# Flamingo block with gated cross attention and hyper-connections: the high part of normalized x made by ScalarE from x itself, and five finished weight and value tiles as row tiles of the tail

## The chip, the cores and the metric

The kernel runs on one core of a Trainium2 chip. The metric is the device time of one execution in microseconds (us). The engines are PE (TensorE; its weight loads are PEld), DVE (VectorE), ACT (ScalarE), POOL (GpSimd) and SP (SyncE, which issues nearly all transfers). L275 means line 275 of the kernel.

## What is computed

The reference takes x of 8 batches, 512 rows d and 2048 columns s, and a context of the same shape. Two gated steps follow each other:

```python
x = x + tanh(g_xattn) * xattn(layernorm(x), ctx, mask, ...)
x = x + tanh(g_ffn)   * ffn(layernorm(x), ...)
```

- xattn: in patches of 128 columns, q and k come from the normalized x by 256x512 weights, the values from the context; 8 heads of 32 attend within a patch; gelu, an output projection and the mask follow.
- ffn: each row of 2048 is four streams of 512. From the normalized row come 16 + 4 + 4 logits. The 16 become a 4x4 mixing matrix by 50 Sinkhorn iterations (temperature 0.1), blended with the identity; the others are softmaxed to weights `H_pre` and `H_post`. The output is the mixed streams plus `H_post` times a 512x512 branch of the `H_pre` sum.

Everything is float32. The layer norm runs along s, so its mean and scale belong to a row d, which is a partition of a tile.

## The kernel before

The main loop walks over 32 blocks of 512 columns (4 per batch), each in four steps t of one patch; a string of letters (`ORDER`) fixes which pieces are emitted in each step. These pieces are prepared up to three blocks ahead. The order on each engine's queue is not the program's: the launch code builds with a scheduler that simulates a timeline (`schedule_with_timeline_sim=True`, L1210) and takes the pieces by priority, mostly that of program order, as their inputs and buffers come free. Tiles of one tag share as many buffers as `bufs` says, and a new tile of that tag waits until the oldest is free.

What the change and the steps of the prediction touch:

- `proj(n)` (L260): q and k of block n. Each product is made of float16 parts: normalized x is split into a high part xh and a low part xl = xn - xh, and PE adds three products per chunk of 128 rows (L288 to L290). For each of the 4 chunks c, POOL makes xn = x * rstd + nb in float32 (L270; ACT does so for two chunks of the first block, L268), ACT casts xn to float16 (L275), and POOL subtracts (L277; DVE for the two). xn has `BUF_XNP` = 2 buffers, xh and xl have `BUF_XHP` = 4 each. ACT and DVE then take the result from PSUM as two halves (L292, L293).
- `vproj` (L322) makes the values of two patches with the weights `Wv` into `VF[0]` or `VF[1]`; `attv` (L626) reads them. `smax`, `expo` (L333, L614) make the scores, `mh` (L350) carries the row maximum back to the stacked q.
- `outp` (L648): gelu on ACT, o times the mask on POOL (L658), transposes (L667), the output projection and x1 = x + its result, stored to memory.
- `ffn` (L741): the Sinkhorn chain of a batch on DVE (sums and reciprocals) and POOL (products, L870 and L876; DVE for the last batch), with an exponential on ACT every ten sweeps. It ends in `Et` and, for TensorE's chunks, a copy through memory into `HR` (L911, L913).
- The mix of a batch: four chunks of 128 rows, each either on VectorE (`mixv`, L935) or on TensorE (`mixp`, L983). `PE_MIX` gives TensorE one chunk of batch 4, all of batches 5 and 6 and three of batch 7. These 12 chunks are emitted after the main loop, in the tail, with the rest of VectorE's chunks.
- In `mixp` a chunk is read again as 4 tiles xc of 128x512 (SP, L995), ACT adds the mean (L996), PE makes the weighted sum (L997), ACT copies it out (L1000), PE transposes it (L1004), `branch` splits it by ACT and DVE (L927, L928) and multiplies (L931 to L933), ACT copies it out (L1015). Then for each of 4 groups g PE adds two products in PSUM (L1030, L1031), ACT writes the row tile w with a bias (L1033), and SP stores it (L1034). The row tile takes turns: even g in the tag "e32" (2 buffers, which hold the exponentials in the main loop), odd g in the tag "eh" (1 buffer).

Of the kernel before, what the change touches and what calls it, by code (L numbers as in the profile page):

```python
# [9 lines left out]
F32 = mybir.dt.float32  # L10
# [3 lines left out]
AF = mybir.ActivationFunctionType  # L14
# [5 lines left out]
P = 128  # L20
# [19 lines left out]
BUF_GP = 1  # L40
BUF_OP = 1
BUF_XHP = 4
BUF_XNP = 2
BUF_XTP = 4
BUF_CTP = 2
BUF_QDP = 3
# [14 lines left out]
BUF_W = 2  # L61
# [3 lines left out]
BUF_EP = 2  # L65
BUF_XPRE = 1
PSTEPS = (0,1,1,2)
SP0 = 1
XH_POOL = lambda c: False
CAP = 1.0  # L70
NORM0 = True
D_MH = 0
# [26 lines left out]
def gated_xattn_mhc_kernel(  # L99
# [21 lines left out]
    V, A, G, T, SY = nc.vector, nc.scalar, nc.gpsimd, nc.tensor, nc.sync  # L121
# [6 lines left out]
    def ctile(shape, dt, name):  # L128
        return const.tile(shape, dt, tag=name, name=name)
# [16 lines left out]
    WqkH = ctile([P, 4, 512], F16, "WqkH")  # L146
    WqkL = ctile([P, 4, 512], F16, "WqkL")
    Wv = ctile([P, 4, DK], F32, "Wv")
# [35 lines left out]
    xsp = ctx.enter_context(tc.tile_pool(name="xsp", bufs=2))  # L184
    xnp = ctx.enter_context(tc.tile_pool(name="xnp", bufs=BUF_XNP))
    xhp = ctx.enter_context(tc.tile_pool(name="xhp", bufs=BUF_XHP))
# [3 lines left out]
    ep = ctx.enter_context(tc.tile_pool(name="ep", bufs=BUF_EP))  # L190
# [6 lines left out]
    VF = [ctile([P, 2, DK], F32, f"VF{i}") for i in range(NV)]  # L197
# [5 lines left out]
    def defer(k, tag, fn):  # L203
        if k == 0:
            fn()
        else:
            late.append([k, fn, tag])
# [13 lines left out]
    rstd1 = {}  # L221
    nb1 = {}
# [37 lines left out]
    def proj(n):  # L260

        b, k = divmod(n, NBLK)
        xt = xtile[n]
        hs, ls = [], []
        for c in range(4):
            xn = xnp.tile([P, BLK], F32, tag="xn", name="xn")
            if n == 0 and c > 1:
                A.activation(xn, xt[c], AF.Identity, scale=rstd1[b][:, c : c + 1], bias=nb1[b][:, c : c + 1])  # L268
            else:
                G.tensor_scalar(xn, xt[c], rstd1[b][:, c : c + 1], nb1[b][:, c : c + 1], ALU.mult, ALU.add)  # L270
            h = xhp.tile([P, BLK], F16, tag="xh", name="xh")
            if XH_POOL(c):
                G.tensor_copy(h, xn)
            else:
                A.copy(h, xn)  # L275
            l = xhp.tile([P, BLK], F16, tag="xl", name="xl")
            (V if n == 0 and c > 1 else G).tensor_tensor(l, xn, h, ALU.subtract)  # L277
            hs.append(h)
            ls.append(l)
        if NORM0:  # L280
            yield
        qd = qdp.tile([2, 4, 2, P, BLK], F16, tag="qd", name="qd")
        qds[n] = qd
        for m in range(4):
            ps = ps_p.tile([P, BLK], F32, tag="p", name="qk")
            ms = slice(m * P, (m + 1) * P)
            for c in range(4):
                T.matmul(ps, WqkH[:, c, ms], hs[c], start=(c == 0), stop=False)  # L288
                T.matmul(ps, WqkH[:, c, ms], ls[c], start=False, stop=False)  # L289
                mm = T.matmul(ps, WqkL[:, c, ms], hs[c], start=False, stop=(c == 3))  # L290
            ev = evp.tile([P, 2, BLK], F16, tag="ev", name="ev")
            ae = A.activation(ev[:, 0, :], ps, AF.Identity, bias=bqs[:, m : m + 1])  # L292
            ve = V.scalar_tensor_tensor(ev[:, 1, :], ps, bqs[:, m : m + 1], ev[:, 0, :], ALU.add, ALU.subtract)  # L293
            defer(D_QD, "qd", lambda m=m, ev=ev: SY.dma_start(qd[m // 2, 0:2, m % 2].rearrange("t p s -> p t s"), ev))
            if n == LASTN and m == LASTM:
                last.update(pe=mm, act=ae, dve=ve)
            yield
# [59 lines left out]
    with tc.tile_pool(name="set", bufs=1) as st:  # L357
# [99 lines left out]
        for _ in proj(0):  # L457
            pass
# [24 lines left out]
        with tc.issue_after(sd_[0].ins):  # L483
            load_x(NBLK)
        ctload(1)
        pj = proj(1)
        for _ in range(4 if NORM0 else 3):
            next(pj)
# [61 lines left out]
    fp = ctx.enter_context(tc.tile_pool(name="fp", bufs=2))  # L550
# [366 lines left out]
    def mix(b, maps):  # L917
        E, cst, pre, prc, post, rec, HR = maps
        for c in range(4):
            if c in PE_IN[b - B]:  # L920
                yield from mixp(b, c, maps, True)
            elif c not in PE_MIX[b - B]:
                yield from mixv(b, c, maps)

    def branch(pt, ph, pl, y):

        A.copy(ph, pt)  # L927
        V.tensor_tensor(pl, pt, ph, ALU.subtract)  # L928
        yield 1
        for e in range(4):  # L930
            T.matmul(y, ph[:, e, :], WbH[:, e, :], start=(e == 0), stop=False)  # L931
            T.matmul(y, ph[:, e, :], WbL[:, e, :], start=False, stop=False)
            T.matmul(y, pl[:, e, :], WbH[:, e, :], start=False, stop=(e == 3))  # L933

    def mixv(b, n, maps):  # L935
# [31 lines left out]
        for i in range(4):  # L967
# [12 lines left out]
            defer(D_OUT if live[0] else 0, "out", lambda i=i, w=w: SY.dma_start(out[b, n * P : (n + 1) * P, 512 * i : 512 * i + 512], w))  # L980
            yield 1

    def mixp(b, n, maps, inp=False):  # L983

        E, cst, pre, prc, post, rec, HR = maps
        rows = x1s[b].rearrange("d (j e) -> (d j) e", j=4)
        orow = out[b].rearrange("d (j e) -> (d j) e", j=4)
        PD = f1.tile([P, 4, 32], F32, tag="PD", name="PD", bufs=2)
        G.tensor_tensor(PD, blk.unsqueeze(1).broadcast_to([P, 4, 32]), rec[:, 4 * n : 4 * n + 4, 0:1].broadcast_to([P, 4, 32]), ALU.mult)
        xc = []  # L990
        xps = (ps_t if inp else ps_p).tile([P, 512], F32, tag="t" if inp else "p", name="xpp")
        for g in range(4):
            q = 4 * n + g
            t = fp.tile([P, 512], F32, tag="x1", name="xc", bufs=BUF_X1) if inp else xp_.tile([P, 512], F32, tag="xt", name="xc")
            SY.dma_start(t, rows[q * P : (q + 1) * P, :])  # L995
            A.activation(t, t, AF.Identity, bias=rec[:, q, 1:2])  # L996
            T.matmul(xps[32 * g : 32 * g + 32, :], PD[:, g, :], t, start=True, stop=True)  # L997
            xc.append(t)
        xs = fp.tile([P, 512], F32, tag="xpre", name="xps", bufs=BUF_XPRE) if inp else xp_.tile([P, 512], F32, tag="xt", name="xps")
        A.copy(xs, xps)  # L1000
        yield 1
        pt = (ps_t if inp else ps_p).tile([P, 4, P], F32, tag="t" if inp else "p", name="xpT")
        for e in range(4):
            T.transpose(pt[:, e, :], xs[:, e * P : (e + 1) * P], ident)  # L1004
        y = ps_t.tile([P, 512], F32, tag="t", name="yp")
        if inp:
            ph = fp.tile([P, 4, P], F16, tag="ph", name="ph", bufs=BUF_PH)
            pl = fp.tile([P, 4, P], F16, tag="pl", name="pl", bufs=BUF_PH)
        else:
            ph = xhp.tile([P, 4, P], F16, tag="xh", name="phb")  # L1010
            pl = xhp.tile([P, 4, P], F16, tag="xl", name="plb")
        for r in branch(pt, ph, pl, y):
            yield r
        ys = fp.tile([P, 512], F32, tag="pj", name="ys", bufs=BUF_PJ) if inp else xp_.tile([P, 512], F32, tag="xt", name="ys")
        A.copy(ys, y)  # L1015
        yield 1
        QD = xtp.tile([P, P, 4], F32, tag="xTt", name="QD")
        G.tensor_tensor(QD, ident.unsqueeze(2).broadcast_to([P, P, 4]), post[:, n, :].unsqueeze(1).broadcast_to([P, P, 4]), ALU.mult)
        HD = xtp.tile([P, 4, 32, 4], F32, tag="xTt", name="HD")
        G.tensor_tensor(  # L1020
            HD,
            blk.unsqueeze(1).unsqueeze(3).broadcast_to([P, 4, 32, 4]),
            HR[:, 4 * n : 4 * n + 4, :].unsqueeze(2).broadcast_to([P, 4, 32, 4]),
            ALU.mult,
        )
        pw = None if inp else [ps_s.tile([P, 2, 512], F32, tag="s", name="mx") for _ in range(2)]
        for g in range(4):
            q = 4 * n + g
            ps = ps_t.tile([P, 512], F32, tag="t", name="mx1") if inp else pw[g // 2][:, g % 2]
            T.matmul(ps, QD[:, 32 * g : 32 * g + 32].rearrange("p t i -> p (t i)"), ys, start=True, stop=False)  # L1030
            T.matmul(ps, HD[:, g].rearrange("p t i -> p (t i)"), xc[g], start=False, stop=True)  # L1031
            w = fp.tile([P, 512], F32, tag="w", name="w", bufs=BUF_W) if inp else ep.tile([P, 512], F32, tag="eh" if g % 2 else "e32", name="wp", bufs=1 if g % 2 else BUF_EP)
            A.activation(w, ps, AF.Identity, bias=rec[:, q, 2:3])  # L1033
            SY.dma_start(orow[q * P : (q + 1) * P, :], w)  # L1034
            yield 1
# [178 lines left out]
```

## Time and profile before

| what | us |
|---|---|
| median of 3 runs | 1701.85 |
| lowest and highest run | 1693.76, 1705.0 |
| the profiled execution, its own time | 1693.74 |
| span in its trace | 1692.0 |
| main loop's last values product (L642) | 1487.64 |
| first row tile of the tail (L1033) | 1516.05 |
| Sinkhorn of batch 6 ends (store of Et, L911) | 1590.97 |
| Sinkhorn of batch 7 ends (store of Et, L911) | 1645.06 |
| last store issued (L980) | 1689.05 |

The profile is of one execution; times inside it count from the start of its span. A line of the waits reads: engine and line that stood idle, what released it, us in total, times, the longest. A line of the timeline reads: start, duration, engine, line, operation, output and inputs, and in brackets the idle time before it and what ended that. A group of instructions gives count, busy time, mean duration in ns and the idle time ahead of it.

### The profile page before, as it was taken

What the parts mean: (1) busy time and instruction counts of PE and PEld (TensorE: products, weight loads), DVE (VectorE), ACT (ScalarE), POOL (GpSimd) and SP (SyncE); (2) the same over time, 40 slices, a digit from 0 to 9 for tenths busy, and PEclk for the clock granted to TensorE, in tenths of its full rate; (3) what the DMA queues carried; (4) which work ended last, traced back from release to release, by engine and by line L of the source; (5) the groups of instructions that cost most, each with busy time, mean ns of one, the idle gap of its engine ahead of it and who ended that gap; (6) DMA issues with size and microseconds to landing.
All of it is one profiled execution on the core that took longest, in us unless ns stands there. A gap on an engine that the chain in (4) does not pass through costs nothing.

```text
span 1692.0 us, 32528 instructions
## 1 busy us (share of the span) xinstructions
PE 1487.1 (88%) x10453; PEld 880.8 (52%) x10517; DVE 1201.6 (71%) x3552; ACT 1065.3 (63%) x2046; POOL 818.6 (48%) x1158
## 2 busy tenths in 40 slices
PE   4899989999997988988898988888798999778887
PEld 2555546556655655555555554545455556543233
DVE  7634334666776679868777777777788889878872
ACT  3356475667657666686568765686566667555454
POOL 1322233544454465656466654656557655643211
PEclk9899999999999999999999999999999999899999
DMA  6789897787588556876589664876556575334443
GB/s 202 206 234 276 252 257 182 199 242 219 158 240 232 168 173 196 258 228 204 151 237 281 204 176 137 260 230 179 172 164 203 179 206 148 96 107 143 135 157 125
DMA packets 317656, 330.61 MB, mean 195 GB/s; under 512 B 50535, under 2 KB 215719, under 8 KB 317486
## 3 DMA queue, kind: packets, MB, share of 16 engines
q1 hardware_dynamic: 316238, 328.20, 66.0%
q8 instruction: 83, 1.36, 0.4%
q14 instruction: 87, 0.71, 0.1%
q10 hardware_dynamic: 1248, 0.33, 0.1%
HBM read 226.71 MB, written 101.16 MB: 194 GB/s over the span
## 4 chain that ended last, share of the span: by engine, by line
PE 38%; DVE 20%; DMA 14%; ACT 10%; issue 9%; POOL 8%; SPq 1%; another core or an unknown queue 0%; POOLq 0%; ACTq 0%; DVEq 0%
PE vp L330 5%; DMA xs<-in_x_dram 4%; PE qk L288 3%; PE qk L290 3%; PE qk L289 3%; DVE w L976 3%; PE op L693 2%; DMA out_dram<-w 2%; PE lgx L564 2%; PE op L694 2%; PE op L695 2%; PE u L642 2%; PE u L638 2%; PE smax L340 2%; DMA xt<-in_x_dram 2%
## 5 line engine op out<-in xcount | busy, mean ns | idle before, releaser
L330 PE MATMUL vp<-Wv,ct 128*128 128x256 f32 x1024 | 253.0, 398 | 17.5 <-DMA ct<-in_cx_dram 8.7
L330 PEld LDWEIGHTS vp<-Wv,ct 128*128 128x128 f32 x1024 | 198.0, 199 | 54.4 <-DMA ct<-in_cx_dram 9.5
L876 POOL TENSOR_TENSOR W<-E,uv 128x64 f32<-128x64 f32 x343 | 115.6, 340 | 220.4 <-DVE uv L874 86.3
L976 DVE SCALAR_TENSOR_TENSOR w<-x,Et,w 128x512 f32<-128x512 f32 x180 | 182.8, 1017 | 34.0 <-POOL w L974 24.7
L288 PE MATMUL qk<-xh,WqkH 128*128 128x512 f16 x512 | 196.9, 386 | 11.2 <-DVE ev L293 8.6
L277 POOL TENSOR_TENSOR xl<-xn,xh 128x512 f16<-128x512 f32 x126 | 155.3, 1243 | 97.3 <-ACT xh L275 96.0
L289 PE MATMUL qk<-xl,WqkH 128*128 128x512 f16 x512 | 197.3, 386 | 2.9 <-POOL xl L277 2.9
L290 PE MATMUL qk<-xh,WqkL 128*128 128x512 f16 x512 | 197.3, 385 | 0.0
L870 POOL TENSOR_TENSOR W<-E,uv 128x64 f32<-128x64 f32 x308 | 105.3, 345 | 165.6 <-DVE uv L880 70.9
L343 DVE TENSOR_REDUCE smax<-smax 128x8 f32<-128x1024 f32 x128 | 156.2, 1221 | 39.4 <-PE smax L340 32.3
L623 ACT ACTIVATE e<-sT,ebi,esc 128x1024 f32<-128x1024 f32 x128 | 153.6, 1200 | 22.1 <-PE sT L621 21.9
L878 DVE TENSOR_REDUCE sm<-W 128x16 f32<-128x64 f32 x392 | 99.7, 257 | 84.9 <-POOL W L876 80.2
L293 DVE SCALAR_TENSOR_TENSOR ev<-qk,bqs,ev 128x512 f16<-128x512 f32 x128 | 94.3, 738 | 57.5 <-ACT ev L292 56.5
L693 PE MATMUL op<-gh,WoH 128*128 128x512 f32 x256 | 119.3, 468 | 17.5 <-DVE ev L293 9.5
L699 ACT ACTIVATE junk<-xt,nmean 128x512 bf16<-128x512 f32 x128 | 92.0, 719 | 66.9 <-DVE xt L697 30.4
L270 POOL TENSOR_SCALAR xn<-xt,ln_r,nb 128x512 f32<-128x512 f32 x126 | 115.5, 920 | 36.5 <-DVE nb L254 28.2
L292 ACT ACTIVATE ev<-qk,bqs 128x512 f16<-128x512 f32 x128 | 86.8, 679 | 66.8 <-PE qk L290 66.3
L658 POOL TENSOR_TENSOR o<-o,mb 128x1024 f32<-128x1024 f32 x32 | 76.0, 2375 | 100.0 <-ACT o L653 99.3
L872 DVE TENSOR_REDUCE sm<-W 128x16 f32<-128x64 f32 x352 | 74.4, 214 | 58.9 <-POOL W L870 55.4
L974 POOL TENSOR_TENSOR w<-w,pj 128x512 f32<-128x512 f32 x60 | 78.3, 1306 | 75.4 <-ACT w L969 42.9
L340 PE MATMUL smax<-KS,QS 97*128 97x128 f16 x1024 | 86.5, 226 | 31.4 <-ACT mh L350 14.2
L697 DVE TENSOR_TENSOR xt<-op,xt 128x512 f32<-128x512 f32 x128 | 86.9, 679 | 36.6 <-remote 22.6
(289 smaller groups left out, 3503.3 us busy)
## 6 DMA issues: line engine op xcount, KB each, us to landing
xt<-in_x_dram SPq DMA_DIRECT2D x128, 256.0 KB
ct<-in_cx_dram SPq DMA_DIRECT2D x64, 512.0 KB
qd<-ev SPq DMA_DIRECT2D x128, 256.0 KB
xTt<-in_xT_dram SPq DMA_DIRECT2D x128, 256.0 KB
x1s<-xt SPq DMA_DIRECT2D x128, 256.0 KB
xs<-in_x_dram SPq DMA_DIRECT2D x112, 256.0 KB
QS<-qd SPq DMA_DIRECT2D x192, 128.0 KB
KS<-qd SPq DMA_DIRECT2D x192, 128.0 KB
```

Of the source, the lines that this page charges most:

```text
L270: G.tensor_scalar(xn, xt[c], rstd1[b][:, c : c + 1], nb1[b][:, c : c + 1], ALU.mult, ALU.add)
L277: (V if n == 0 and c > 1 else G).tensor_tensor(l, xn, h, ALU.subtract)
L288: T.matmul(ps, WqkH[:, c, ms], hs[c], start=(c == 0), stop=False)
L289: T.matmul(ps, WqkH[:, c, ms], ls[c], start=False, stop=False)
L290: mm = T.matmul(ps, WqkL[:, c, ms], hs[c], start=False, stop=(c == 3))
L330: T.matmul(ps[:, h, :], ct[:, c, h * P : (h + 1) * P], Wv[:, c, :], start=(c == 0), stop=(c == 3))
L340: T.matmul(sc[:, h, :], q[0:97, h, sl], kk[0:97, h, sl], start=True, stop=True)
L343: V.tensor_reduce(mx, sc, AX.X, ALU.max)
L623: A.activation(e32, sc, AF.Exp, bias=ebi[:, t : t + 1], scale=esc[:, t : t + 1])
L693: T.matmul(ps, WoH[:, e, cs], gh[:, e], start=(e == 0), stop=False)
L876: (G if SK_POOL(b - B + 8) else V).tensor_tensor(W4[:, h], E4[:, h], ub[:, h], ALU.mult)
L976: V.scalar_tensor_tensor(w, x1[j], E[:, n, 4 * j + i : 4 * j + i + 1], w, ALU.mult, ALU.add)
```

## The change

There are two parts. In `proj` the high part xh is no longer a cast of xn: ACT computes x * rstd + nb from x and writes it as float16, so it does not depend on xn. POOL still makes xn and the difference. xn has one buffer instead of two; an unused switch goes.

In `mixp`, for chunks of the tail, the row tile w comes from a rota of eight instead of the two tags: half of `WqkH` and of `WqkL` seen as float32, half of `Wv`, `VF[0]`, `VF[1]`, then "eh" once and "e32" twice. The five tiles hold weights and values that the main loop reads and the tail does not.

```diff
-BUF_XNP = 2
+BUF_XNP = 1
...
-XH_POOL = lambda c: False
...
             h = xhp.tile([P, BLK], F16, tag="xh", name="xh")
-            if XH_POOL(c):
-                G.tensor_copy(h, xn)
-            else:
-                A.copy(h, xn)
+            A.activation(h, xt[c], AF.Identity, scale=rstd1[b][:, c : c + 1], bias=nb1[b][:, c : c + 1])
...
+    spare = [WqkH.bitcast(F32)[:, 0:2, :], WqkL.bitcast(F32)[:, 0:2, :], Wv[:, 0:2, :], VF[0], VF[1]]
+    turn = [0]
+
+    def tailw(g):
+        k = turn[0] % (len(spare) + 3)
+        turn[0] += 1
+        if k < len(spare):
+            return spare[k].rearrange("p c e -> p (c e)")
+        return ep.tile([P, 512], F32, tag="eh" if k == len(spare) else "e32", name="wp", bufs=1 if k == len(spare) else BUF_EP)
...
-            w = fp.tile([P, 512], F32, tag="w", name="w", bufs=BUF_W) if inp else ep.tile([P, 512], F32, tag="eh" if g % 2 else "e32", name="wp", bufs=1 if g % 2 else BUF_EP)
+            w = fp.tile([P, 512], F32, tag="w", name="w", bufs=BUF_W) if inp else tailw(g)
```

## The prediction

> **What bounds the kernel now.** I read the page's totals and slices first, then the chain that ended last, then the waits by engine for 300 to 1400 us, then the tail after the main loop.
>
> ```profile
> PE 1487.1 (88%) x10453; PEld 880.8 (52%) x10517; DVE 1201.6 (71%) x3552; ACT 1065.3 (63%) x2046; POOL 818.6 (48%) x1158
> PE   4899989999997988988898988888798999778887
> ACT  3356475667657666686568765686566667555454
> PE 38%; DVE 20%; DMA 14%; ACT 10%; issue 9%; POOL 8%; SPq 1%; another core or an unknown queue 0%; POOLq 0%; ACTq 0%; DVEq 0%
> ```
>
> PE is busy in eight or nine tenths of nearly every slice and carries the largest part of the chain; ACT is busy 63% and carries 10%, POOL 48% and 8%. No single engine is saturated: PE is held up by many short waits. So work that is moved between ACT and POOL is worth what PE waits for it, not what it lasts. These are the waits around the changed lines, over the whole span (us, times, longest):
>
> ```profile
> POOL xl L277 <- ACT xh L275: 96.0, 29, 17.0
> ACT xh L275 <- POOL xn L270: 19.9, 18, 2.5
> PE smax L340 <- ACT mh L350: 14.2, 9, 3.8
> PE vp L330 <- ACT VF L331: 6.1, 4, 2.6
> PE qk L289 <- POOL xl L277: 2.9, 4, 1.1
> PE qk L288 <- ACT xh L275: 1.2, 1, 1.2
> ```
>
> POOL stands 96.0 us at the subtraction for the high part, and ACT 19.9 us for the normalized row, but PE waits only 2.9 + 1.2 = 4.1 us for either part. The waits by window say that 77.1 of the 96.0 us fall before 300 us, where POOL has little else (57.98 us busy from 100 to 300 us); 19.0 us are left from 300 to 1400 us.
>
> In the tail TensorE's chunks go through PE, ACT and the store. Here is ACT, and then SP's queue, in one chunk:
>
> ```profile
> 1654.22 0.69 ACT L1033 ACTIVATE wp<-mx,rec 128x512 f32<-128x512 f32 x1 [0.17 <-PE mx L1031]
> 1656.38 0.69 ACT L1033 ACTIVATE wp<-mx,rec 128x512 f32<-128x512 f32 x1 [0.99 <-PE mx L1031]
> 1659.21 0.69 ACT L1033 ACTIVATE wp<-mx,rec 128x512 f32<-128x512 f32 x1 [2.15 <-DMA out_dram<-wp]
> 1663.06 1.46 ACT L996 ACTIVATE xc<-xc,rec 128x512 f32<-128x512 f32 x2 [1.79 <-DMA xc<-x1s]
> ```
>
> ```profile
> 1654.07 6.18 SPq L1034 DMA_DIRECT2D out_dram<-wp  x4
> 1660.35 1.82 SPq L995 DMA_DIRECT2D xc<-x1s  x4
> ```
>
> The row tile of an odd g has one buffer: the second row was written by 1654.91, the fourth could start at 1659.21, 4.3 us later, when the store had landed. Behind it on SP stand the loads of the next chunk (issued at 1660.35), and ACT then waits for them. The waits from 1591 to 1692 us give the sum:
>
> ```profile
> ACT wp L1033 <- DMA out_dram<-wp: 6.9, 4, 2.1
> PEld mx L1030 <- ACT wp L1033: 7.1, 8, 1.5
> ```
>
> **The high part on ScalarE.** The 128 casts at L275 are replaced by 128 activations that read x with a scale and a bias per partition. The trace has both prices:
>
> ```profile
> L275 ACT CAST xh<-xn x128: 602/617/639, 30.1 to 1377.9; 128x512 f16<-128x512 f32 x128
> L969 ACT ACTIVATE w<-x,sm,Et 128x512 f32<-128x512 f32 x80 | 64.3, 812 | 47.5 <-DMA out_dram<-w 44.9 <-DVE xt L697 1.7 <-DVE Et L899 0.7
> ```
>
> The mean of L275 in the groups by line is 614 ns. L969 is the same shape with two operands per partition: 812 ns (L268, the two such activations at the start, 814). So each costs 812 - 614 = 198 ns more, and 128 x 0.198 = 25.3 us of ACT are added. Taken away are the 19.9 us for which ACT stood at POOL's xn. Net 25.3 - 19.9 = +5.4 us of ACT. ACT carries 10% of the chain, so I take 0.1 x 5.4 = 0.5, rounded up to +1 us, since the operations that PE does wait for (mh, VF) queue behind it in order. Bounds: +25.3 if all of the dearer form lies on the path and no wait comes back, -19.9 if the waits come back whole and the form is hidden.
>
> **The subtraction on POOL.** xl still needs both xn and xh. xh no longer comes after xn, so ACT can be done first. The 77.1 us before 300 us are idle time and pay nothing; of the 19.0 later, PE sees part of its 4.1 us. I take -2 us, bounds -19.0 and 0 (xl waits for nothing that it did not wait for before). What is late next for POOL is xn itself, or the xh buffers, which PE's last qk releases (ACT waited for that 2.9 us).
>
> **One xn buffer.** Before, POOL can run two xn ahead of the xh that it waits for; now xn of chunk c+1 comes after xl of chunk c, both on POOL, so it waits for no further engine there, but one xn more stands after the release of xh: 0.77 us (median of L270) in each of 32 blocks, 24.6 us in all. Its cover is that PE comes for xl later than POOL delivers it, in all but 4 places. Behind it on POOL stand the iteration's products (L870, L876) and o times mask (L658). I take +1 us, bounds 0 (the same work with less freedom gains nothing by itself) and +24.6. At the start two xn are made on ACT; with one buffer they alternate with DVE's xl, against which the first xh comes up to 1.2 us sooner (PE's wait for it). The first ACT xn would move from 32.02 to the end of xl at 33.10. I take 0, bounds -1.2 and +1.1.
>
> **Eight row tiles instead of three in the tail.** No instruction is added: 48 activations and 48 stores stay, and a row waits for the store eight rows back. Four rows took SP 6.18 us in the rows above, so eight take some 12, against a return of 4.3: the 6.9 us of ACT go. Which of the four reach the end? The last (1.54 us before 1686.21) does not: the final store is that of VectorE's chunk, issued at 1689.05. The one of 2.15 us holds back the loads at 1660.35, ACT's xc and PE's xpp: 2 us. Two of 1.52 and 1.68 us, near 1605 and 1613, have PE work of another chunk beside them: 1 us. I take -3 us, bounds -6.9 and +2.2, the latter if stores that leave sooner hold up a chunk's loads by as much as ACT's longest wait for xc in the tail (2.2, before 1618.93). The tiles are free in time: the last qk was at 1417 us, the last u, which reads VF, at 1487.64, the first row at 1516.05, so the new tiles add no wait for their old readers. What is late next is PE: per chunk it waits about 0.7 us each for xps, phb and ys, and those are not touched.
>
> A rule from the Trainium skill, Perfetto Trace Analysis, section Identifying the Most-Contended Engine: matmul busy time is a poor measure, weight-load busy time a better one. The tail has 57.83 us of weight loads in 185 us against 158.07 us of matmul; by the rule PE has room, all 6.9 us would come through, and the sum below would be 4 us lower. I go by the rows instead: f16 matmuls of 512 columns start 0.215 us apart without a gap, so PE follows its own queue there.
>
> **Sum.** +1 - 2 + 1 + 0 - 3 = -3 us. The profiled execution took 1693.74 us (span 1692.0 and 1.7 around it), so it would take 1691. The three runs have a median of 1701.85 and a spread from 1693.76 to 1705.0; the profile is at their lower end. From the median the sum gives 1699. I predict the middle, 1695 us; alone this case reaches from 1685 to 1702.
>
> **Rivals.** What both need is in the launch code: the order on each engine is chosen when the program is built, by a scheduler that simulates its timeline, so a cheaper or dearer step can move others.
>
> Slower: the dearer activation pushes what PE waits for. ACT is busy 138 of 200 us between 700 and 1300 us, and there PE already waits for mh 14.2 and VF 6.1 us. If all 25.3 us reach PE and no wait returns: 1701.85 + 25.3 = 1727. It decides from 17 us (1%), two thirds of it. Against it: the 19.9 us that ACT gets back.
>
> Faster by over 1%: ACT, rid of POOL, serves PE's other waits sooner. From 300 to 1400 us ACT waited 13.0 us for xn; if all comes through, with the whole 6.9 us of the tail and 1.2 at the start, that is 21.1 us: 1693.74 - 21.1 = 1673, or 1681 from the median. Against it: PE's waits for mh lie at 1007 to 1220 us, mostly not beside a wait for xn.
>
> Nothing: the tail's waits move to the chain of batch 7, whose Et comes at 1645 whatever the rows do, and the first part is hidden: 1702.
>
> **Chances.** Forecast 0.38 and nothing 0.12, together within 1%, which is about what a measurement of this kernel can tell from no change: 0.50. Faster by over 1%: 0.28. Slower by over 1%: 0.22. The range takes in both outer cases but for their ends: 1671 to 1726.
>
> **What would show it.** L275 becomes an activation of about 0.81 us; ACT's wait for xn at that line is gone; POOL's wait for xh falls below 20 us after 300 us; no wp waits for a store; the loads of the last chunk's xc are issued about 2 us sooner after its rows. I am wrong if PE's waits for mh, VF or xl grow by more than 10 us, if the loop's end (the last u, 1487.64) moves by more than 10 us, or if wp waits for a weight tile's last reader.

## The result, and the profile after

The kernel became slower. Its median is 1721.38 us (1714.26 to 1724.92, 4 runs) against 1700.98 us beside it; the ratio is 1.0118, with a 95% interval from 1.0092 to 1.0143. My forecast of -3 us had the wrong sign. The profiled execution took 1724.92 us (span 1723.1, against 1692.0). It is the longest of its four, and the one before is the shortest of its four: the medians lie 20.4 us apart, the two traces 31.1. The granted TensorE clock is the same in both, 0.958 and 0.959.

Ahead of line 276 the lines of the changed kernel lie up to 3 lower (L275 is now L272, L277 is L274), from there to 980 3 lower, and after that 8 higher. First the page's totals, slices and chain, to be laid beside those of before:

```profile
PE 1494.9 (87%) x10455; PEld 886.5 (51%) x10517; DVE 1199.6 (70%) x3552; ACT 1081.5 (63%) x2044; POOL 815.4 (47%) x1158
PE   4898989998998998889897888888788888778887
ACT  3366475758556776687568667686577666654444
PE 36%; DVE 19%; DMA 17%; ACT 9%; issue 9%; POOL 7%; SPq 1%; POOLq 0%; ACTq 0%; another core or an unknown queue 0%; DVEq 0%
```

No engine has much more to do: ACT is busy 16.2 us longer (1081.5 against 1065.3), PE 7.8, POOL 3.2 less. The span grew by 31.1. So most of the loss is waiting. The changed line itself, in the groups (count, busy time, mean ns, idle time ahead of it):

```profile
L272 ACT ACTIVATE xh<-xt,nb,ln_r 128x512 f16<-128x512 f32 x128 | 99.0, 803 | 5.9 <-PE qk L287 5.3 <-DMA x1s<-xt 0.4
```

It is the activation I priced: 803 ns against 614, so 189 x 128 = 24.2 us. The 19.9 us for which ACT stood at POOL's xn are gone; its idle time is now 5.3 us for PE's last qk, which frees an xh buffer. These are the waits of the span around the changed lines:

```profile
POOL xl L274 <- ACT xh L272: 88.3, 20, 22.2
PE op L690 <- DVE ev L290: 24.4, 14, 3.4
PE smax L337 <- ACT mh L347: 16.2, 9, 3.0
PE vp L327 <- ACT VF L328: 15.1, 7, 3.7
PE qk L285 <- DVE ev L290: 10.1, 7, 3.2
PE vp L327 <- DVE ev L290: 8.0, 4, 4.4
PE op L690 <- DVE xt L694: 7.3, 6, 2.6
ACT xh L272 <- PE qk L287: 5.3, 9, 1.4
PE qk L286 <- POOL xl L274: 1.7, 3, 0.7
```

PE's wait for the low part stays small, 1.7 us. What grew are waits at op, vp and qk. These three kinds of tile share two buffers of PSUM (the tag "p"), and each can start when ACT or DVE has taken an earlier one out (ev, VF, xt). Before, these rows read:

```profile
PE op L693 <- DVE ev L293: 9.5, 11, 2.2
PE qk L288 <- DVE ev L293: 8.6, 6, 2.5
PE vp L330 <- ACT VF L331: 6.1, 4, 2.6
PE op L693 <- DVE xt L697: 2.6, 4, 1.0
```

All such rows together are 30.5 us before and 65.5 after; all rows of PE's idle time are 194.2 and 217.5. When the first exponential of a block starts says where the time was lost (after minus before, profiled executions): +10 us at block 4, +22 at block 8, +26 at block 11, +18 at 16, +15 at 24, +22 at 31. The loop's last values product starts at 1512.30 instead of 1487.64: some 25 us are lost in the main loop, and about 6 in the tail. The first third looks worst, but it is no sign of the single buffer: a kernel with two buffers, below, is as late there.

The tail's rows wait for no store any more. Here is its end after the change (timeline: SP's queue and ACT):

```profile
1672.31 0.39 SPq L908 DMA_DIRECT2D hd<-Et  x1
...
1704.22 0.59 ACT L924 CAST ph<-xpT 128x512 f16<-128x512 f32 x1 [1.14 <-PE xpT L954]
...
1716.04 0.69 ACT L1041 ACTIVATE wp<-mx,rec 128x512 f32<-128x512 f32 x1 [0.23 <-ACT pj L970]
```

The last row came 1.54 us late for a store before; now it follows ACT's own work. But Et of batch 7 is stored at 1672.31, 27.3 us later than before, and the mix of batch 7 needs it.

### The profile page after: what moved, and what is told of

It is laid out like the page before. It is cut to its first block, busy times and chain, and to the rows that moved or that the text cites. A ratio compares the mean times of both kernels' runs of the same rounds, so it can differ in the third digit from the quotient of the medians.

```text
span 1723.1 us, 32546 instructions
## 1 busy us (share of the span) xinstructions
PE 1494.9 (87%) x10455; PEld 886.5 (51%) x10517; DVE 1199.6 (70%) x3552; ACT 1081.5 (63%) x2044; POOL 815.4 (47%) x1158
## 4 chain that ended last, share of the span: by engine, by line
PE 36%; DVE 19%; DMA 17%; ACT 9%; issue 9%; POOL 7%; SPq 1%; POOLq 0%; ACTq 0%; another core or an unknown queue 0%; DVEq 0%
DMA xs<-in_x_dram 5%; PE vp L327 5%; DVE w L973 3%; PE qk L285 3%; PE op L690 3%; PE qk L286 3%; PE qk L287 2%; DMA out_dram<-w 2%; DMA x<-x1s 2%; PE op L691 2%; PE op L692 2%; PE lgx L561 2%; DVE smax L340 2%; PE u L639 2%; DMA x1s<-xt 2%
## 5 line engine op out<-in xcount | busy, mean ns | idle before, releaser
L327 PE MATMUL vp<-Wv,ct 128*128 128x256 f32 x1024 | 259.9, 406 | 31.4 <-ACT VF L328 15.1
L327 PEld LDWEIGHTS vp<-Wv,ct 128*128 128x128 f32 x1024 | 201.8, 203 | 72.2 <-ACT VF L328 18.1
L274 POOL TENSOR_TENSOR xl<-xn,xh 128x512 f16<-128x512 f32 x126 | 154.3, 1225 | 110.1 <-ACT xh L272 88.3
L285 PE MATMUL qk<-xh,WqkH 128*128 128x512 f16 x512 | 196.0, 383 | 11.9 <-DVE ev L290 10.1
L973 DVE SCALAR_TENSOR_TENSOR w<-x,Et,w 128x512 f32<-128x512 f32 x180 | 175.1, 973 | 43.7 <-POOL w L971 27.4
L690 PE MATMUL op<-gh,WoH 128*128 128x512 f32 x256 | 120.7, 473 | 31.9 <-DVE ev L290 24.4
L269 POOL TENSOR_SCALAR xn<-xt,ln_r,nb 128x512 f32<-128x512 f32 x126 | 110.9, 880 | 66.9 <-DVE nb L253 32.1
L600 ACT ACTIVATE xs<-xs,nmean 128x512 f32<-128x512 f32 x112 | 80.0, 715 | 49.8 <-DMA xs<-in_x_dram 38.9
L691 PE MATMUL op<-gl,WoH 128*128 128x512 f32 x256 | 107.5, 420 | 0.7 <-POOL gl L680 0.7
```

The costliest lines, as they stand in the source:

```text
L327: T.matmul(ps[:, h, :], ct[:, c, h * P : (h + 1) * P], Wv[:, c, :], start=(c == 0), stop=(c == 3))
L690: T.matmul(ps, WoH[:, e, cs], gh[:, e], start=(e == 0), stop=False)
L691: T.matmul(ps, WoH[:, e, cs], gl[:, e], start=False, stop=False)
L973: V.scalar_tensor_tensor(w, x1[j], E[:, n, 4 * j + i : 4 * j + i + 1], w, ALU.mult, ALU.add)
```

## Experiments

The theory after the two traces: **one buffer for xn** makes the normalization of a block longer, and PE pays for it at other places than xl. Rivals: **the dearer activation** (my slower rival), **the high part's independence from xn**, which changes what ACT does when, and **the luck of the order**: the build chooses each engine's order by a simulated timeline, and any edit draws a new one. Every ratio below is against the kernel before, with its 95% interval.

### The two parts apart

`p1_only` has the first part alone (new high part, one xn buffer, the old row tiles); `p2_only` only the rota of eight:

```diff
-            w = ... else ep.tile([P, 512], F32, tag="eh" if g % 2 else "e32", ...)
+            w = ... else tailw(g)
```

> First part alone: the high part made by ScalarE from x, one xn buffer; the tail's row tiles as before. My theory: the main loop lost some 21 to 25 us by its end (the last values product moved from 1487.6 by that much) and the tail 6 to 7 us more, and the first part owns the loop's share, so 1.009 to 1.015 of the time before, the tail from the last output projection on as long as before. Rival (the tail's rota owns the loss): 1.000 to 1.004.

> Second part alone: the rota of eight row tiles in the tail, the cast and two xn buffers as before. My theory: the main loop is untouched, and in the tail PE stands at batch 6's first rows for HR, before the next chunk is prepared, so 1.003 to 1.006 of the time before although no row waits for a store. Rival (as the prediction has it): 3 us gained, 0.998.

Measured: p1_only 1.0109 [1.0078, 1.0139], p2_only 1.0005 [0.9985, 1.0025]. The whole loss lies in the first part. PE's order is that of the changed kernel in p1_only (all but 4 of 10,455 matmuls); p2_only keeps the main loop's order of before. Even so its last values product starts 5.6 us later in its profiled execution (1493.21): two executions of one order can differ by that much. The rota brings +0.9 us with an interval from -2.6 to +4.3, not the -3 I forecast, and less than the 1.003 to 1.006 expected here. The timeline of its tail's end:

```profile
1650.75 0.38 SPq L911 DMA_DIRECT2D hd<-Et  x1
...
1680.71 0.58 ACT L927 CAST ph<-xpT 128x512 f16<-128x512 f32 x1 [1.13 <-PE xpT L957]
...
1692.52 0.69 ACT L1043 ACTIVATE wp<-mx,rec 128x512 f32<-128x512 f32 x1 [0.23 <-ACT pj L973]
```

and the same cast before:

```profile
1673.07 0.59 ACT L927 CAST ph<-xpT 128x512 f16<-128x512 f32 x1 [0.54 <-PE xpT L957]
```

This cast begins the branch of VectorE's last chunk, whose store ends the kernel. From it to the end of the span there are 18.9 us in all three kernels (1692.0 - 1673.07, 1699.6 - 1680.71, 1723.1 - 1704.22). The cast waits for PE's transposition (in brackets): from batch 7's Et (1645.06, 1650.75, 1672.31) to the cast it takes 28.0 us before, 30.0 in p2_only, 31.9 after. The rows no longer wait, but the transposition that the end hangs on does not come sooner after Et. Why it comes 2 to 4 us later was not followed further.

### The second buffer back, and one buffer alone

`p1_xn2` and `both_xn2` are p1_only and the changed kernel with `BUF_XNP = 2`; `xn1_only` is the kernel before with

```diff
-BUF_XNP = 2
+BUF_XNP = 1
```

> First part with two xn buffers, tail as before. If the one xn buffer owns the loop's loss (24.6 us was its upper bound), 1.000 to 1.004; if the dearer activation or the new order does, the same as the first part alone within 0.5%, 1.008 to 1.016.

> The cast from xn stays, only the xn buffers go from two to one, tail as before. If the buffer matters by itself: slower, 1.005 to 1.015, and more than with the new high part, as ACT's cast then also holds the buffer. If it doesn't: 0.997 to 1.003.

> Both parts, but two xn buffers. If the one buffer owns the loss: 1.000 to 1.005 of the time before, as the first part with two buffers was 1.0014. If the two parts cost something together that neither costs alone: 1.008 or more.

Measured: p1_xn2 1.0014 [0.9989, 1.0039], both_xn2 1.0021 [0.9995, 1.0046], xn1_only 1.0144 [1.0106, 1.0183]. One number in the kernel makes the loss come and go: 1.0118 - 1.0021 is 0.97%, 16.5 us, with an interval from 0.6 to 1.3% if the two half-widths add as squares; 1.0109 - 1.0014, measured side by side, is 0.95%. But that number also draws a new order: between the two kernels of such a pair some 1400 of the 10,455 matmuls stand elsewhere in PE's order.

Where does a pair lose? both_xn2 is as late as the changed kernel in the first two thirds (+27 us at block 8, +29 at 11, +17 at 16, against before), and then gains (+12 at 24, +10 at 31). From the first exponential of block 20 to the end of the loop's last values product it takes 528.9 us, the changed kernel 546.5; p1_xn2 takes 523.0, p1_only 542.2. So in these pairs the single buffer loses against its twin in the last twelve blocks. In xn1_only the path is seen at work (waits over the span):

```profile
POOL xl L277 <- ACT xh L275: 166.7, 70, 19.7
ACT xh L275 <- POOL xn L270: 31.2, 25, 3.9
PE qk L288 <- ACT xh L275: 10.8, 11, 2.7
PE qk L289 <- POOL xl L277: 4.5, 7, 1.8
```

With the cast, xn, xh, xl and the next xn now follow each other between two engines: POOL stands at xh 70 times instead of 29, ACT at xn for 31.2 us instead of 19.9, and PE waits 15.3 us for the two parts instead of 4.1. From the start of a block's first xh to that of its last xl the mean is 9.0 us before and 15.8 in xn1_only. With the new high part it is 8.0 with two buffers and 9.8 with one: xh is there ahead of xn, and POOL merely alternates xn and xl. So there the delay is 1.8 us a block, and it is not seen where PE waits for xl.

### The dearer activation, and the missing wait

`price` keeps the dependence on xn and two buffers, and pays the dearer form (scale 1 and bias 0 from tiles). `dep` is p1_xn2 with a plain cast of x, the cheap form without the dependence; its high part is of x that is not normalized.

```diff
-                A.copy(h, xn)
+            A.activation(h, xn, AF.Identity, scale=onesb[:, 0:1], bias=zb[:, 0:1])   # price
+            A.copy(h, xt[c])                                                         # dep
```

> The kernel before with the dearer form alone: the high part is still made from xn, but as an activation with a scale of 1 and a bias of 0 from operands per partition. 128 times 188 ns, 24 us more of ACT, with the old wait for xn. If ACT's time reaches the end: 1.007 to 1.014; if it is hidden: 0.996 to 1.004.

> The kernel before, with the cast taken from x instead of from xn (the high part is then not normalized): the cheap form with the new freedom from xn, two buffers. It frees ACT of 17 to 20 us of waits and adds nothing. If the freedom is worth something at the end: 0.990 to 0.997; if it is hidden: 0.998 to 1.005.

Measured: price 0.9989 [0.9966, 1.0012], dep 1.0135 [1.0103, 1.0167]. The group in price:

```profile
L274 ACT ACTIVATE xh<-xn,zb,onesb 128x512 f16<-128x512 f32 x128 | 100.8, 805 | 19.7 <-POOL xn L272 17.0 <-PE qk L289 2.4
```

The 191 ns x 128 = 24.4 us are paid by ACT and not by the kernel. That rival fell. But dep, with two buffers, the cheap form and no wait of ACT for xn, lost 1.35%. My theory does not explain that; so either the missing dependence is a cause, or a new order alone can cost this much.

### What an order is worth

To draw other orders at almost no work, one block of the value projection is copied into VF a second time by ScalarE, 0.6 us once:

```diff
         A.activation(VF[i % NV], ps, AF.Copy, scale=1.0 / S_UNIT)
+        if i == 9: A.activation(VF[i % NV], ps, AF.Copy, scale=1.0 / S_UNIT)
```

`nudge_before`, `nudge_after` and `nudge_xn2` are the kernel before, the changed one and both_xn2 with this line.

> The kernel before, with one more copy of the values from PSUM by ACT in the tenth vproj (0.6 us of work, once). The build then gives some 1300 of PE's 9952 rows another place. If the loss is the luck of a new order, this may move by 0.5% or more either way; if the one buffer is a cause of its own, 0.996 to 1.004.

> The changed kernel with the same one copy more: another order, the same single xn buffer. If the one buffer is the cause it stays at 1.008 to 1.016 of the time before; if the changed kernel only had a bad order, it may fall to 1.000 to 1.005.

> Both parts with two xn buffers, and the one copy more in the tenth vproj, which gives some 1100 of PE's rows another place. A third new order with two buffers. If one buffer is the cause: 0.998 to 1.006, like the other two-buffer kernels. If orders differ by as much as the change itself: outside of that.

Measured: nudge_before 1.005 [1.0019, 1.0081], nudge_after 1.0102 [1.0067, 1.0137], nudge_xn2 1.0012 [0.9985, 1.0039]. Compared with the order without it, the copy moves some 1200 to 1550 of PE's 10,450 matmuls, about as many as the second buffer does, and it shifts the kernel before by 0.5%, some 8 us for 0.6 us of work. The pair with one and two buffers stays apart, and again the difference arises in blocks 20 to 31: 538.1 us with one buffer, 518.8 with two.

### The PSUM buffers as the place

If the loss is paid at the two buffers of the tag "p", it should go when the values product takes its tile from another tag. `vpt_xn1` and `vpt_xn2` are the changed kernel and both_xn2 with

```diff
-        ps = ps_p.tile([P, 2, DK], F32, tag="p", name="vp")
+        ps = ps_t.tile([P, 2, DK], F32, tag="t", name="vp")
```

> The changed kernel, with the values' PSUM tile taken from the other ring (tag t) instead of the ring that q, k and the output projection use. The kernels with one xn buffer wait some 53 us for that ring's tiles on PE, those with two some 32. If that ring is where the one buffer costs, this one loses less against its twin with two buffers than 0.97%: 0.5% or less. If not, the difference stays at about 1%. Both may move together, since the other ring gets fuller.

> The twin with two xn buffers, values in the other ring too. Against the kernel before 0.995 to 1.01; what counts is the distance to the twin with one buffer: 0.5% or less if the shared ring is the place of the loss, 1% if not.

Measured: 1.0356 [1.0322, 1.039] and 1.0393 [1.0354, 1.0432]. The waits at "p" fell to 19.2 and 11.7 us, but the tag "t" is worse for the values. The waits of vpt_xn1:

```profile
PE gTp L664 <- POOL o L655: 56.2, 20, 6.7
PE smax L337 <- ACT e L620: 21.5, 9, 6.3
```

In this arrangement a single xn buffer costs nothing (-0.4%, interval -0.9 to +0.2). That the buffers of "p" are the place was not shown: the experiment moved too much else. The clock is part of that. Its mean is 0.931 and 0.926 here, against 0.959 before: the records of the traces show TensorE at half its clock for 242 and 263 us, against 141. In such a stretch before (534 to 540 us, after a wait of 6.8 us) matmuls of qk start 0.43 us apart instead of 0.215. By estimate that alone is worth at most half of the additional time, 51 and 61 us of the 61 and 67 lost; whether the waits bring the low clock or follow from it was not tested.

### The buffer in other orders

Four more halves of pairs: `price_xn1` is price with one buffer; `nudge_xn1only` is nudge_before with one; `nudge2_after` and `nudge2_xn2` copy at i == 2 in the changed kernel and in both_xn2.

> The kernel price (the cast of xn with the dearer form of activation) with one buffer for xn in place of two: the partner with two buffers stands at 0.999. Theory 'one buffer costs by itself': 1.009 to 1.016, waits of PE for ring p up from 36 to 58 us or more. Rival 'luck of the order': 0.997 to 1.006 is as likely as 1.01, the waits stay under 50 us.

> The kernel before with one buffer for xn and, beside it, one extra copy of the tenth block of the value projection into VF by ScalarE (0.6 us of work, the same nudge as in nudge_before): one more order with one buffer, whose partner with two buffers is nudge_before (1.005). Theory 'one buffer costs by itself': ratio 1.010 to 1.020, the waits of PE for the shared ring p (qk, vp, op) at 58 us or more. Rival 'luck of the order': the ratio can lie anywhere from 0.999 to 1.015, and the pair's difference may have either sign.

> The changed kernel with one extra copy of the third block of the value projection into VF by ScalarE: one more order with one buffer. Theory 'one buffer costs by itself': 1.008 to 1.016 and the waits for ring p at 58 us or more. Rival 'luck of the order': anywhere from 0.998 to 1.015, as far from its partner nudge2_xn2 in one direction as in the other.

> The same as nudge2_after with two buffers for xn. Theory 'one buffer costs by itself': 0.998 to 1.005, about 0.9% under nudge2_after, waits for ring p under 52 us. Rival 'luck of the order': it may lie above nudge2_after as well as under it.

Measured: price_xn1 1.0288 [1.0262, 1.0313], nudge_xn1only 1.0118 [1.0091, 1.0146], nudge2_after 0.9977 [0.9957, 0.9997], nudge2_xn2 0.9979 [0.9947, 1.0011]. In nudge2_after one buffer costs nothing, and the kernel is 1.4% faster than the changed one that it differs from by one useless copy. Yet the delay on POOL is there: 10.1 us from first xh to last xl against 7.9 in nudge2_xn2, 2.2 us a block. So that delay alone does not make the loss. Blocks 20 to 31 take 528.6 us against 522.9, and what is lost there had been gained before. The waits of nudge2_after:

```profile
PE vp L327 <- ACT VF L328: 13.5, 8, 3.3
PE op L691 <- DVE ev L290: 13.3, 13, 2.5
PE qk L285 <- DVE ev L290: 12.4, 8, 2.2
PE qk L286 <- POOL xl L274: 2.1, 4, 0.7
POOL xl L274 <- ACT xh L272: 106.6, 23, 21.9
```

In price_xn1, the slowest of the four, PE waits 23.7 us for the two parts:

```profile
PE qk L287 <- ACT xh L274: 13.0, 13, 3.4
PE qk L288 <- POOL xl L276: 10.7, 13, 1.7
```

The waits at "p" are 53.0 us in nudge2_after and were 53.0 in nudge_before (1.005), and only 33.7 in price_xn1. So this sum, on which all four expectations leaned, does not tell a fast order from a slow one. All of PE's waits together do so better: 190.9 us in nudge2_after, 223.2 in price_xn1, though nudge_after lost 1% with 193.7.

The last two runs: `nudge4_after` copies at i == 4 in the changed kernel, `nudge_dep` at i == 9 in dep.

> The changed kernel with one extra copy of the fifth block of the value projection into VF by ScalarE: a fourth order of the changed kernel's main loop with one buffer (so far 1.0118, 1.0102 and 0.9977). Theory 'the single buffer costs about 1% unless the order happens to suit it': 1.007 to 1.015. Rival 'it is the luck of the order alone': anywhere between 0.997 and 1.015, with no pull towards 1.01.

> The kernel dep (two buffers, high part as a plain cast of x, so it is not normalized; it stood at 1.0135) with one extra copy of the tenth block of the value projection into VF by ScalarE. If dep's loss was the luck of its order: 0.997 to 1.006, as the other kernels with two buffers. If it comes from the high part not waiting for xn (ScalarE free of GpSimd, a cause of its own that the changed kernel has too): 1.010 to 1.016 again.

Measured: nudge4_after 1.0056 [1.003, 1.0082], nudge_dep 1.0014 [0.9993, 1.0034]. The first lies under the 1.007 to 1.015 of the theory and within the range of the rival; its twin with two buffers was not run. The second says that dep's loss of 1.35% was its order: 0.6 us of extra work took it away, and the missing dependence does not cost this by itself.

### All together

One buffer minus two, pair by pair (interval from the two half-widths):

| high part | order | two buffers | one buffer | difference, % |
|---|---|---|---|---|
| cast | as built | 1 (before) | 1.0144 | +1.4 (1.1 to 1.8) |
| cast | copy at 9 | 1.005 | 1.0118 | +0.7 (0.3 to 1.1) |
| cast, dearer form | as built | 0.9989 | 1.0288 | +3.0 (2.6 to 3.3) |
| new | as built | 1.0021 | 1.0118 | +1.0 (0.6 to 1.3) |
| new, old row tiles (p1), nearly the orders of the line above | as built | 1.0014 | 1.0109 | +0.95 (0.6 to 1.3) |
| new | copy at 9 | 1.0012 | 1.0102 | +0.9 (0.5 to 1.3) |
| new | copy at 2 | 0.9979 | 0.9977 | 0.0 (-0.4 to +0.4) |
| new, vp in "t" | as built | 1.0393 | 1.0356 | -0.4 (-0.9 to +0.2) |

What is settled: the loss belongs to the step from two buffers to one together with the order that the build then makes; the second buffer brings back 0.97 of the 1.18%. Leaving out the two kernels with vp in "t", nine of the ten kernels with two buffers lie at 1.005 or under, and seven of the eight with one at 1.0056 or over, so one buffer does cost in most orders (some of these kernels share an order). With the cast it cost something in three pairs of three, and there the trace shows a round trip: PE's waits for the two parts rise from 4.1 to 15.3, from 4.1 to 14.6 and from 3.7 to 23.7 us. With the new high part they rise by no more than 2 us in any pair. What stays open: for the new high part the price depends on the order, from nothing to 1%, and it can't be said how much of it is the buffer's own and how much the draw, since the two kernels of a pair never share an order. With two buffers a draw can lose as much (dep). I also can't name the one wait at which the 16.5 us are paid.

## Why the prediction was wrong, step by step

- **The step that failed: "One xn buffer", taken as +1 us** because "its cover is that PE comes for xl later than POOL delivers it, in all but 4 places". The second buffer's return is worth 16.5 us (10 to 23) in the order as built. The upper bound that I wrote down, +24.6, holds it. The cover was real at its own line (PE's wait for xl is 1.7 us, before 2.9), but that line was the wrong place to look: the time is lost elsewhere, in blocks 20 to 31 against the twin with two buffers. The delay per block was also larger than the 0.77 us of one xn, 1.8 us. My reading is that the order is built around when the parts come, so that a longer stage on POOL puts other work in other places; the runs do not show this, and in the order of nudge2_after 2.2 us of delay a block cost nothing.
- **A term put at nothing: the new order.** The rivals name it, the sum has no term for it. The runs show an order alone moving a kernel by up to 1.4% (the changed kernel against nudge2_after), several times the -3 us of the sum.
- **The dearer form**: predicted 198 ns x 128 = 25.3 us of ACT; it was 189 x 128 = 24.2, and price shows it hidden. The +1 taken for it was about right (-1.9 us by the ratio, -5.8 to +2.0). The rival "slower by over 1%" came true in its number and not in its cause, which was this activation; that the range up to 1726 holds 1721.38 is luck, since that rival set its upper end. The ScalarE price of an operand per partition also stands in the Trainium skill (ScalarE: Activation LUTs, section What ACT_TABLE_LOAD costs): about 93 ns for each. By estimate that is 186 for two, which agrees with the 189 here.
- **ACT's wait for xn and POOL's for xh**: the first went to nothing, as said. The second fell from 19.0 to 13.1 us between 300 and 1400 us. Both gave no time back: 1.0014 and 1.0021 with two buffers, where I had taken -2 for POOL; a gain of 2 us is just about the lower end of the first interval and outside the second.
- **The tail, taken as -3 us**: p2_only says +0.9 (-2.6 to +4.3). The four waits went, as said. That the last one would not reach the end was right, and the others did not reach it either, because VectorE's last chunk, which I had named for that one alone, sets the end for all of them, behind a transposition on PE. My rival "nothing", with batch 7's Et, described this better than my forecast did, though Et did not stay at 1645.
- **The weighing of the skill's rule** (Perfetto Trace Analysis, Identifying the Most-Contended Engine, on matmul busy time): I took PE in the tail to follow its own queue, and set the rule aside. An estimate from the trace before: if each matmul is counted up to the start of the next one, but at most by the tenth percentile of that spacing for its line and shape, 1113 us of the 1692 are matmuls in flow and 561 are gaps; of the tail's 185 us they are 122 and 55. So the trace agrees with the rule, and PE had room. But the gain that I had worked out from it, all 6.9 us of the rows' waits, did not come either: in p2_only the waits went and the end did not come sooner.
- **"The main loop's end moves by more than 10 us"** was named as what would make me wrong, and it did: by 24.7 in the traces (1487.64 to 1512.30).
- **The method**: I added terms measured in the old order. Each edit drew a new order, and a draw alone moves this kernel by up to 0.5% without any buffer changed (nudge_before) and 1.2% (dep against nudge_dep). Against that, a sum of -3 us said little; the sign had to come from what costs in most orders, and that was the buffer.

## What to carry to other kernels

A buffer taken from a short stage could not be priced here by the wait at its own consumer, since the scheduler built a new order with it: count how much longer the stage's chain of engines becomes per iteration, as a warning and not as a price, and look for the loss anywhere in the loop, against the twin that differs in the buffer alone. Before an effect of 1% is given a cause, run the pair that differs in the one edit, in two or three orders drawn by a harmless extra instruction; a single pair can show the draw. In this tail waits that did not lie ahead of what the last store hangs on gave nothing back: follow the chain back from the last store first.

## What was not expected

- One copy of 0.6 us changed the kernel before by +0.5% [+0.2, +0.8] and dep from 1.0135 to 1.0014, by the order alone.
- 24 us more of ACT, an engine busy 63%, cost nothing (price, 0.9989), while a second buffer of 2 KB per partition, with the order that it brings, decided 16.5 us.
- The same single buffer cost 3.0% under the dearer form with the cast's dependence, against 1.4% under the plain cast. That the longer xh lies in the round trip of one buffer and not of two would explain it; no run here tells that from the luck of its order.
